# Routed two-of-eight expert kernel: a load gate tied to a gather's issue, and two single-tile scatter-adds moved behind gathers

## The chip, the cores and the metric

The kernel runs on one NeuronCore of a Trainium2 chip. The metric is device time of one execution in microseconds (us). Before the change it is 449.95 us, the median of three runs (449.35 to 451.89 us).

## What is computed

There are 4096 tokens (64 sequences of 64) of 256 numbers each. For every token a gate picks two of eight experts and gives each a weight; an expert is three dense layers (256 to 512, 512 to 512, 512 to 256), the first two with a relu. The output is the token plus the weighted sum of its two experts. The reference computes all eight experts for all tokens and gives six of them the weight zero:

```
var = jnp.mean(x * x, axis=-1, keepdims=True)
xn = rms_w * (x * jax.lax.rsqrt(var + EPS))
gate = xn @ wg_W + wg_b + (genre_embed @ gg_W + gg_b)
gate_w = jax.nn.softmax(gate, axis=-1)
topk_w, topk_i = jax.lax.top_k(gate_w, TOP_K)
cw = jnp.sum(jax.nn.one_hot(topk_i, E, dtype=x.dtype) * topk_w[..., None], axis=-2)
h1 = jax.nn.relu(jnp.einsum('bsh,ehm->bsem', x, W1) + b1)
h2 = jax.nn.relu(jnp.einsum('bsem,emn->bsen', h1, W2) + b2)
out_e = jnp.einsum('bsen,enh->bseh', h2, W3) + b3
return x + jnp.einsum('bseh,bse->bsh', out_e, cw)
```

(The last line joins the reference's last sum and its residual.) All arithmetic here is in float32.

## The kernel before, in words

**Tiles and units.** The kernel computes only the chosen pairs of token and expert. Pairs of one expert are collected in tiles of 128 token rows. Units 0 to 7 are single tiles, one for each expert, filled from the first 1024 tokens; they run while the other 3072 tokens are still being routed. From unit 8 (`E` in the code) on, a unit is up to four tiles of one expert, and its layers 1 and 2 are computed with seven block products in place of eight (class `Fast`); unit 8 is the first unit of four.

**What a unit needs.** Its rows of `x` come by an indirect DMA that GpSimd (POOL) issues, one for each tile (`gather` for units 0 to 7 into `xg`, `gather_unit` from unit 8 on into `xgE` or `big`; line 864). One more indirect DMA per tile fetches the eight gate weights of each token (`gather_cw`, tile `cg`, line 864), from a small array in DRAM (`cwdA` for units 0 to 7, `cwdR` from unit 8 on) that POOL wrote before (line 444); these are the column gathers of the change. Expert weights come by DMAs on SyncE's queue (SP) for the first units: layer 1 in the ring `w1r`, layer 2 in `w2a`, which keeps all eight experts, layer 3 in the ring `w3r`. From unit 8 on the rows go by SP through DRAM to be transposed: `stow` writes them to `scr` (line 904), `shuffle` reads them back into `gTs` (line 911), and VectorE (DVE) transposes blocks of `gTs` into `xT` (line 920).

**What a unit gives.** `give` scales the unit's result into `ys` or `xg` on DVE (line 1328) and adds each tile to the output rows in DRAM with an indirect DMA on POOL, the scatter-add (line 1329). Before any adds the output must hold the residual: `fill(k)`, k from 0 to 3, copies a quarter of the remaining rows of `x` to the output with a DMA of 768 KB on SP (line 1428). A scatter-add reads a row and writes it back, so each one waits until the scatter-adds of the unit before it have landed (the loop over `behind`); the first one of unit 8 waits for all fills too.

**The order.** The program is written out by hand in the order of each engine (`manual_schedule`). `first_part`, `gather(0)`, `other_loads`, `gather(1)` and `second_part` follow each other; then come `head_step(u)` for units 0 to 6, `step(7)`, and `step_fast(u)` from unit 8 on. Each engine takes its instructions in this order, so an instruction that waits holds all that stand behind it on its engine. Two waits concern the change:

- In `other_loads` (line 573) the first load on SP, `loads[2]`, which is layer 1 of expert 1 into `w1r`, waits until the first gather (`fetches[0]`, the rows of unit 0) has landed. All other weight loads stand behind it on SP.
- The `give` of unit 5 stands at the end of `head_step(6)`, that of unit 6 at the end of `step(7)`. Unit 8's column gathers (`gather_cw(8)` in `step(7)`) stand behind the first on POOL, unit 10's row gathers (`fetches_of(8)` in `step_fast(8)`) behind the second. `fill(3)` stands ahead of unit 10's `stow` on SP and waits for the last of unit 8's column gathers (`columns[E]`).

Of the kernel before, what the change touches and what calls it, by code (L numbers as in the profile page):

```python
# [11 lines left out]
F32 = mybir.dt.float32  # L12
# [3 lines left out]
ALU = mybir.AluOpType  # L16
# [36 lines left out]
def kernel(  # L53
# [53 lines left out]
    orows = out.rearrange("b s h -> (b s) h")  # L107
# [16 lines left out]
    def ring(pool, shape, tag, bufs, b, dt=F32):  # L124
# [32 lines left out]
        out=tri, in_=ones16, pattern=[[1, P]], compare_op=ALU.is_gt, fill=0.0, base=0, channel_multiplier=-1  # L157
# [4 lines left out]
        out=ntri, in_=ntri, pattern=[[1, P]], compare_op=ALU.is_ge, fill=0.0, base=0, channel_multiplier=-1  # L162
# [31 lines left out]
    idxR = const.tile([P, NREST], I32, name="idxR")  # L194
    ebt = const.tile([P, 1], I32, name="ebt")
    nex = const.tile([P, 1], I32, name="nex")
    vT = const.tile([P, 2, E, MC], F32, name="vT")


# [252 lines left out]
    fills, loads, fetches, fetched = [], [], [], []  # L452
# [119 lines left out]

    def other_loads():


        load_weights(1, (0,))
        tc.add_manual_dep(
            loads[2].ins,
            fetches[0].ins.name,
            mybir.DependencyInfo(mybir.DependencyClass.Sync, mybir.DependencyReason.DATA),  # L580
            reason="the first tile's rows go first",
        )
        load_weights(0, (2,))
        load_weights(1, (1,))
        load_weights(2, (0,))
        nc.sync.dma_start(b3_sb[:, 0:2], b3[0:2].unsqueeze(0).to_broadcast([P, 2, H]))
        load_weights(1, (2,))
        load_weights(2, (1,))
# [270 lines left out]
    def index(b):  # L859
        return idxA[:, b : b + 1] if b < E else idxR[:, b - E : b - E + 1]  # L860

    def fetch(dst, src, b):

        return nc.gpsimd.indirect_dma_start(  # L864
            out=dst,
            out_offset=None,
            in_=src,
            in_offset=bass.IndirectOffsetOnAxis(ap=index(b), axis=0),
            bounds_check=NT - 1,
            oob_is_err=False,  # L870
        )
# [13 lines left out]
            fetches.append(fetch(xgR[u % 2][:, k], xrows, b))  # L885

    NCG = 16
    columns = {}
    cgR = buf(run, [P, NCG, E], "cg")

    def gather_cw(u):
        for k, b in enumerate(tiles(u)):
            cg = cgs[b] = cgR[:, turn_of(u, k) % NCG]
            columns[u] = fetch(cg, (cwdA if b < E else cwdR)[:, :], b)

    xT = buf(run, [P, HC, SLOTS, BT], "xT")
    shs = gTf.rearrange("p (s k f) -> p s k f", s=SLOTS, k=P // SQ)
# [415 lines left out]
        n = rows(u, k)  # L1313
        nc.tensor.matmul(sums(u, k)[0:n], lhsT=(quad if n == SQ else both), rhs=y_of(u, k), start=True, stop=True)

    def give(u, which=None, summed=False, written=False):

        bs, cws = tiles(u), ww[u][4]
        if u not in given:
            given[u] = 0  # L1320
            adds.append([])
        for k in which or range(size(u)):
            b = bs[k]
            cw, bc = cws[k]
            n = within(u, k).stop - k * BT
            y = y_of(u, k)
            src = y if summed else sums(u, k)
            V.scalar_tensor_tensor(y[0:n], src[0:n], cw[0:n], bc[0:n], ALU.mult, ALU.add)  # L1328
            add = nc.gpsimd.indirect_dma_start(  # L1329
                out=orows,  # L1330
                out_offset=bass.IndirectOffsetOnAxis(ap=index(b)[0:n], axis=0),
                in_=y[0:n],
                in_offset=None,
                bounds_check=NT - 1,
                oob_is_err=False,
                **({} if written else {"compute_op": ALU.add}),
            )
            if reads and not written:
                tc.declare_no_dep(add.ins, reads[0].ins, reason="the tiles of a unit are of one expert: no token twice")
            if b < E:  # L1340
                for f in fills[1:]:
                    tc.declare_no_dep(add.ins, f.ins, reason="the first E tiles hold tokens of the first part alone")

            behind = list(adds[-2]) if len(adds) > 1 else [fills[0]]
            if b >= E and not behind_fills:
                behind += fills[1:]
                behind_fills.append(b)
            for a in adds[-1]:
                tc.declare_no_dep(add.ins, a.ins, reason="the tiles of a unit are of one expert: no token twice")
            for a in behind:  # L1350
                tc.add_manual_dep(
                    add.ins,
                    a.ins.name,
                    mybir.DependencyInfo(mybir.DependencyClass.Sync, mybir.DependencyReason.DATA),
                    reason="a token's row is read and written back",
                )
            adds[-1].append(add)
            given[u] += 1
        if given[u] == len(bs):
            ww.pop(u)  # L1360

    given = {}
    reads = []
    behind_fills = []
    NF = 4

    def head_step(u, more):

        if u + 3 < E:
            gather(u + 3)  # L1370
        for k in range(3 * u, min(3 * u + 3, E)):
            gather_cw(k)
        table(GC * (NCH - 1) * (u == E - 2))
        layer1(u)
        if u == 0:
            load_weights(u + RING, (0,))
            fills.append(nc.sync.dma_start(our[:, 0:NA, :], xr[:, 0:NA, :]))
            load_weights(u + RING - 1, (2,))
            load_weights(u + RING, (1,))
            nc.sync.dma_start(b3_sb[:, 2:4], b3[2:4].unsqueeze(0).to_broadcast([P, 2, H]))  # L1380
            third_part()
        elif u + RING < E:
            load_weights(u + RING, (0,))
        if u == 0:
            pass
        else:
            transpose_x(u + 1)
            stage_1(u + 1)
            if u == E - 2:
                while not fetched:  # L1390
                    more(1000000)
            elif u != 2:
                more(3200)
            if u > 1:
                scaled(u - 1, "A")
            layer3(u - 1)
            if u - 1 + RING < E:
                load_weights(u - 1 + RING, (2,))
            if u + RING < E:
                load_weights(u + RING, (1,))  # L1400
            if u in (2, 4):
                nc.sync.dma_start(b3_sb[:, u + 2 : u + 4], b3[u + 2 : u + 4].unsqueeze(0).to_broadcast([P, 2, H]))
        table(GC * (u == E - 3))
        if u == 0:
            layer2(u, {1: last_upright, 2: lambda: transpose_x(1)})
            stage_1(1)
            more(3200)
        else:
            more(3200)
            layer2(u)  # L1410
        if u == 1:
            scaled(0, "A")
        if u == E - 2:
            stream_3(E, mybir.EngineType.SP)
            fill(1)
            stream_1(E + 1, mybir.EngineType.SP)
            stow(E + 1)
            shuffle(E + 1)
            give(u - 2)
        if u >= 1 and u != E - 3:  # L1420
            give(u - 1)
        if u == E - 3:
            stream_1(E, mybir.EngineType.SP)
            fill(0)

    def fill(k):
        i = NA + k * (NB // NF)
        f = nc.sync.dma_start(our[:, i : i + NB // NF, :], xr[:, i : i + NB // NF, :])
        for a in sum(adds, []):
            tc.declare_no_dep(f.ins, a.ins, reason="the first E tiles hold tokens of the first part alone")  # L1430
        if k == NF - 1:
            tc.add_manual_dep(
                f.ins,
                columns[E].ins.name,
                mybir.DependencyInfo(mybir.DependencyClass.Sync, mybir.DependencyReason.DATA),
                reason="the weight columns of the first unit go first",
            )
        fills.append(f)

    def fetches_of(u, last):  # L1440
        far = E + 1 < u + 2 < last
        if far:
            gather_unit(u + 2)
            stow(u + 2)
        return far

    def step(u, last):
# [9 lines left out]
            stage_2(u)  # L1457
        if u + 1 < last:
            gather_cw(u + 1)
        if u - 1 >= E:  # L1460
            scales(u - 1)
        if u < last:
# [23 lines left out]
        if u == E - 1:  # L1486
            stream_1(E + 2, mybir.EngineType.SP)
            stream_3(E + 1, mybir.EngineType.SP)
            fill(2)
        give(u - 1)  # L1490
        for _ in folds:
            pass

    def step_fast(u, last):

        if u == E:
            transpose_x(u)
            fill(3)
        far = fetches_of(u, last)
        follows = u + 1 < last  # L1500
        if follows:
            gather_cw(u + 1)
# [188 lines left out]
    with tc.manual_schedule():  # L1691
# [21 lines left out]
        for u in range(E - 1, CUT):  # L1713
# [7 lines left out]
            elif u == CUT - 1:  # L1721
                tc.switch_hint({e: arm for e in ENGS}, len(ARMS), "tail")
            steps(u, u + 1, E + NQT + 1)
    kept = (ww, ex, cgs, given)
    state = [{k: list(v) if isinstance(v, list) else v for k, v in d.items()} for d in kept]
    done = [list(a) for a in adds]
    for k in tc.Switch(arm, len(ARMS), hint="tail"):
# [39 lines left out]
```

## Time and profile before

| | us |
|---|---|
| median of 3 runs | 449.95 |
| the profiled execution | 448.42 |
| its span (first to last instruction) | 446.7 |
| TensorE matmul (PE) busy | 439.6 |
| TensorE weight load (PEld) busy | 409.2 |
| DVE busy | 368.4 |
| ACT busy | 240.0 |
| POOL busy | 279.4 |

The profiled execution has 1.72 us outside its span. In the views, a row of the timeline gives the start in us, the duration in us, engine, line and operation, output from input, and in brackets the idle time of the engine just before with what ended it. Rows of waits give total us, number and longest. Rows of DMA issues give KB and us from issue to landing. Rows of DMA queues give packets, MB, and the share of the 16 DMA engines' time. SPq and ACTq are the issuing side of DMAs; q0 carries what POOL issues, q1 what SP issues. Lines in the profile are those of the kernel before.

### The profile page before, as it was taken

What the parts mean: (1) busy time and instruction counts of PE and PEld (TensorE: products, weight loads), DVE (VectorE), ACT (ScalarE), POOL (GpSimd) and SP (SyncE); (2) the same over time, 40 slices, a digit from 0 to 9 for tenths busy, and PEclk for the clock granted to TensorE, in tenths of its full rate; (3) what the DMA queues carried; (4) which work ended last, traced back from release to release, by engine and by line L of the source; (5) the groups of instructions that cost most, each with busy time, mean ns of one, the idle gap of its engine ahead of it and who ended that gap; (6) DMA issues with size and microseconds to landing.
All of it is one profiled execution on the core that took longest, in us unless ns stands there. A gap on an engine that the chain in (4) does not pass through costs nothing. (4 is left out here: it accounts for less than half of the span.)

```text
span 446.7 us, 9272 instructions
## 1 busy us (share of the span) xinstructions
PE 439.6 (98%) x2967; PEld 409.2 (92%) x2967; DVE 368.4 (82%) x964; ACT 240.0 (54%) x569; POOL 279.4 (63%) x234
## 2 busy tenths in 40 slices
PE   8999999999999999999999999999999999999995
PEld 7699999989889898989899999999999889999994
DVE  6898995698897979797988888887877878889962
ACT  6745544346556564738274646464464465655561
POOL 7854435757887878485765556577647456664323
PEclk9999999999999999999999999999999999999998
DMA  8799999784865857372746464666656555666312
GB/s 311 271 358 385 366 365 380 247 239 133 244 128 160 154 149 164 79 189 70 166 93 141 107 132 111 131 181 135 141 142 141 143 148 104 175 175 169 72 15 50
DMA packets 76015, 78.89 MB, mean 177 GB/s; under 512 B 34991, under 2 KB 64018, under 8 KB 75828
## 3 DMA queue, kind: packets, MB, share of 16 engines
q1 hardware_dynamic: 49408, 43.29, 30.0%
q0 software_dynamic: 14912, 17.60, 22.5%
q10 hardware_dynamic: 11636, 17.32, 12.1%
q8 instruction: 25, 0.41, 0.4%
q14 instruction: 34, 0.28, 0.2%
HBM read 62.73 MB, written 20.12 MB: 185 GB/s over the span
## 5 line engine op out<-in xcount | busy, mean ns | idle before, releaser
L1329 POOL DMA_INDIRECT out_dram<-ys,idxR x59 | 95.7, 1622 | 87.3 <-DVE ys L1328 42.1
L1157 PE MATMUL pb<-hid,big 128*128 128x256 f32 (+7 forms) x456 | 83.4, 326 | 0.0
L1178 ACT ACTIVATE hid<-hid,bb 128x256 f32<-128x256 f32 (+12 forms) x152 | 72.5, 526 | 17.9 <-DVE hid L1175 8.2
L864 POOL DMA_INDIRECT cg<-cwdR,idxR x59 | 66.4, 1125 | 18.0 <-issue 17.4
L1157 PEld LDWEIGHTS pb<-hid,big 128*128 128x128 f32 x456 | 71.4, 191 | 4.7 <-issue 0.8
L1279 PE MATMUL pb<-w3r,hid 128*128 128x256 f32 (+1 forms) x256 | 60.7, 381 | 0.0
L1166 ACT COPY q1s<-pb 128x512 f32<-128x512 f32 (+7 forms) x57 | 27.2, 476 | 60.7 <-PE pb L1157 60.0
L1157 PE MATMUL pb<-mixB,big 128*128 128x256 f32 (+7 forms) x304 | 55.4, 325 | 0.0
L1166 ACT COPY big<-pb 128x512 f32<-128x512 f32 (+7 forms) x57 | 27.1, 476 | 52.3 <-PE pb L1157 52.3
L1157 PE MATMUL pb<-hotA,big 128*128 128x256 f32 (+7 forms) x304 | 52.3, 325 | 0.0
L1279 PEld LDWEIGHTS pb<-w3r,hid 128*128 128x128 f32 (+1 forms) x256 | 46.2, 189 | 6.1 <-issue 0.8
L1157 PEld LDWEIGHTS pb<-mixB,big 128*128 128x128 f32 x304 | 47.9, 191 | 2.6
L1157 PEld LDWEIGHTS pb<-hotA,big 128*128 128x128 f32 x304 | 47.2, 191 | 2.7
L1157 PE MATMUL pb<-mixX,iotx 128*128 128x256 f32 (+7 forms) x228 | 46.3, 326 | 0.0
L864 POOL DMA_INDIRECT xgE<-in_x_dram,idxR x31 | 34.9, 1127 | 11.4 <-issue 8.5
L1157 PEld LDWEIGHTS pb<-mixX,iotx 128*128 128x128 f32 x228 | 37.1, 191 | 2.5 <-ACT q1s L1166 0.2
L864 POOL DMA_INDIRECT big<-in_x_dram,idxR x28 | 32.4, 1157 | 8.5 <-issue 7.0
L1178 ACT ACTIVATE hid<-pb,bb 128x256 f32<-128x256 f32 (+7 forms) x76 | 27.5, 413 | 14.5 <-PE pb L1157 11.4
L1157 PE MATMUL pb<-xT,w1r 128*128 128x256 f32 (+7 forms) x152 | 30.8, 325 | 0.0
L1058 PE MATMUL pb<-hid,w2a 128*128 128x128 f32 x256 | 30.5, 276 | 0.0
L1058 PEld LDWEIGHTS pb<-hid,w2a 128*128 128x128 f32 x256 | 29.7, 192 | 0.7 <-ACT bc L1024 0.4
L920 DVE STREAM_TRANSPOSE xT<-gTs 128x256 f32<-128x256 f32 x55 | 29.0, 632 | 0.0
(341 smaller groups left out, 822.0 us busy)
## 6 DMA issues: line engine op xcount, KB each, us to landing
w3r<-in_L_cond_W_dram ACTq DMA_DIRECT2D x17, 512.0 KB, 5.3
w2a<-in_L_cond_W_dram SPq DMA_DIRECT2D x8, 1024.0 KB, 14.1
w1r<-in_L_cond_W_dram ACTq DMA_DIRECT2D x16, 512.0 KB, 3.5
w1r<-in_L_cond_W_dram SPq DMA_DIRECT2D x11, 512.0 KB, 10.0
w3r<-in_L_cond_W_dram SPq DMA_DIRECT2D x10, 512.0 KB, 11.3
big<-in_x_dram SPq DMA_DIRECT2D x8, 512.0 KB, 6.5
gTs<-scr SPq DMA_DIRECT2D x7, 512.0 KB, 4.8
out_dram<-in_x_dram SPq DMA_DIRECT2D x4, 768.0 KB, 7.1
```

The source lines that it names most:

```text
L864: return nc.gpsimd.indirect_dma_start(out=dst, out_offset=None, in_=src, in_offset=bass.IndirectOffsetOnAxis(ap=index(b), axis=0), bounds_ ...
L920: V.transpose(xT[:, :, s0 + k, :].rearrange("p c (b k) -> p k c b", b=SQ), shs[:, s0 + k].rearrange("p k (a c) -> p k c a", a=SQ),)
L1058: nc.tensor.matmul(ph, lhsT=w2[:, m, ts(n, P)], rhs=hid[0][:, m, 0:BT], start=(m == 0), stop=(m == MC - 1))
L1157: nc.tensor.matmul(bank[:, ts(n, self.w)], lhsT=w[:, c, ts(n, P)], rhs=x[:, c], start=new and n == 0 and c == 0, stop=n == HB - 1 and c == ...
L1166: nc.scalar.copy(self.q[(1, 6, 5).index(k)], self.tall(self.X if k == 5 else self.U))
L1178: nc.scalar.activation(out, src, AF.Relu, bias=ww[self.u][1][:, self.l, n : n + 1])
L1279: nc.tensor.matmul(sums(u, k)[0 : cols.stop - cols.start], lhsT=hid[1][:, n, cols], rhs=w3[:, n, :], start=(i == 0), stop=(i == MC - 1))
L1329: add = nc.gpsimd.indirect_dma_start(out=orows, out_offset=bass.IndirectOffsetOnAxis(ap=index(b)[0:n], axis=0), in_=y[0:n], in_offset=None ...
```

## The change

It has two parts, and the weights, the arithmetic and the number of DMAs stay the same.

**The load gate.** A new tile `shut` of one number per partition is set to zero on POOL (`memset`) between `gather(0)` and `gather(1)`, and `loads[2]` waits for this `memset` in place of the first gather's landing. Since POOL works in order, the `memset` ends behind the issue of the gather. Tiles declared behind `shut` lie a little higher in the on-chip memory.

**The scatter-adds.** `give` is split: the DVE part stays where it was, and the DMA part becomes `send`, which can be held. The `send` of unit 5 is held until `gather_cw(8)` has been issued in `step(7)`; that of unit 6 is held until unit 10's row gathers, `stow(10)` and `fill(3)` have been issued in `step_fast(8)`. There `fill(3)` now stands behind `fetches_of`, and its wait for `columns[E]` is gone.

```
+    shut = const.tile([P, 1], F32, name="shut")
...
     def other_loads():
+        sent = nc.gpsimd.memset(shut, 0.0)
         load_weights(1, (0,))
         tc.add_manual_dep(
             loads[2].ins,
-            fetches[0].ins.name,
+            sent.ins.name,
...
-    def give(u, which=None, summed=False, written=False):
+    def give(u, which=None, summed=False, written=False, held=None):
...
             V.scalar_tensor_tensor(y[0:n], src[0:n], cw[0:n], bc[0:n], ALU.mult, ALU.add)
-            add = nc.gpsimd.indirect_dma_start(
...
+            if held is None:
+                send(u, b, y, n, written)
+            else:
+                held.append((u, b, y, n, written))
...
+    def send(u, b, y, n, written):
+        if u not in opened:
+            opened[u] = True
+            adds.append([])
+        add = nc.gpsimd.indirect_dma_start(
...
         if u >= 1 and u != E - 3:
-            give(u - 1)
+            give(u - 1, held=held if u == E - 2 else None)
...
-        if k == NF - 1:
-            tc.add_manual_dep(
-                f.ins,
-                columns[E].ins.name,
...
         if u + 1 < last:
             gather_cw(u + 1)
+        while held:
+            send(*held.pop(0))
...
-        give(u - 1)
+        give(u - 1, held=held if u == E - 1 else None)
...
         if u == E:
             transpose_x(u)
+        far = fetches_of(u, last)
+        if u == E:
             fill(3)
-        far = fetches_of(u, last)
+        while held:
+            send(*held.pop(0))
         follows = u + 1 < last
         if follows:
             gather_cw(u + 1)
```

Line numbers of the changed kernel are higher by 1 to 12, and tile numbers by one. On POOL, behind the setup, `xg_209` is the target of unit 0's gather and `cw8A` the gate weights of the first 1024 tokens. Before:

```order
L301 IOTA xgE 64x2208 x2
L864 DMA xg_209<-in_x_dram,idxA 128x256
L864 DMA xg_210<-in_x_dram,idxA 128x256
L864 DMA xg_211<-in_x_dram,idxA 128x256
L441 TENSOR_TENSOR cw8A<-ohA,denA 128x64
```

The same place on POOL in the change:

```order
L302 IOTA xgE 64x2208 x2
L866 DMA xg_210<-in_x_dram,idxA 128x256
L576 MEMSET shut 128x1
L866 DMA xg_211<-in_x_dram,idxA 128x256
L866 DMA xg_212<-in_x_dram,idxA 128x256
```

One instruction is new; what stood behind it is one place further down.

On POOL where units 5 to 8 meet, the rows `out_dram<-ys,idxA` are the scatter-adds of units 4 and 5, `out_dram<-xg` those of units 6 and 7, `cg` the column gathers (of unit 8, then of unit 9), `xgE` the row gathers of unit 10, `big` those of unit 11. Before:

```order
L444 DMA cwdR<-cw8B 128x256
L1329 DMA out_dram<-ys,idxA 4096x256 x2
L864 DMA cg<-cwdR,idxR 128x8 x4
L1329 DMA out_dram<-xg_211,idxA 4096x256
L864 DMA xgE<-in_x_dram,idxR 128x256 x4
L864 DMA cg<-cwdR,idxR 128x8 x4
L1329 DMA out_dram<-xg_209,idxA 4096x256
```

The same place on POOL in the change:

```order
L445 DMA cwdR<-cw8B 128x256
L1341 DMA out_dram<-ys,idxA 4096x256
L866 DMA cg<-cwdR,idxR 128x8 x4
L1341 DMA out_dram<-ys,idxA 4096x256
L866 DMA xgE<-in_x_dram,idxR 128x256 x4
L1341 DMA out_dram<-xg_212,idxA 4096x256
L866 DMA cg<-cwdR,idxR 128x8 x4
L1341 DMA out_dram<-xg_210,idxA 4096x256
```

Unit 5's scatter-add moved behind four column gathers, unit 6's behind four row gathers.

On SP at the same time, `out_dram<-in_x_dram` are `fill(2)` and `fill(3)`, `scr` from `xgE` is `stow(10)`, and `gTs` behind it is `shuffle(10)`. Before:

```order
L981 DMA w3r_86<-in_L_cond_W_dram 128x4x256
L1428 DMA out_dram<-in_x_dram 128x1536 x2
L904 DMA scr_187<-xgE 128x16x64
L911 DMA gTs<-scr_187 128x4x256
L1715 TENSOR_LOAD nex
```

The same place on SP in the change:

```order
L982 DMA w3r_86<-in_L_cond_W_dram 128x4x256
L1438 DMA out_dram<-in_x_dram 128x1536
L905 DMA scr_188<-xgE 128x16x64
L1438 DMA out_dram<-in_x_dram 128x1536
L912 DMA gTs<-scr_188 128x4x256
```

`fill(3)` moved from ahead of `stow(10)` to between it and `shuffle(10)`. The instructions of PE, DVE and ACT stand in the order that they had.

More of the change, by code (lines that the diff above doesn't have):

```diff
@@ L578, in other_loads @@
             loads[2].ins,
-            fetches[0].ins.name,
+            sent.ins.name,
             mybir.DependencyInfo(mybir.DependencyClass.Sync, mybir.DependencyReason.DATA),
-            reason="the first tile's rows go first",
+            reason="the first tile's rows are asked for first",
         )
@@ L887 @@
     NCG = 16
-    columns = {}
     cgR = buf(run, [P, NCG, E], "cg")
@@ L893, in gather_cw @@
             cg = cgs[b] = cgR[:, turn_of(u, k) % NCG]
-            columns[u] = fetch(cg, (cwdA if b < E else cwdR)[:, :], b)
+            fetch(cg, (cwdA if b < E else cwdR)[:, :], b)
     xT = buf(run, [P, HC, SLOTS, BT], "xT")
@@ L1314, in joined @@
         nc.tensor.matmul(sums(u, k)[0:n], lhsT=(quad if n == SQ else both), rhs=y_of(u, k), start=True, stop=True)
-    def give(u, which=None, summed=False, written=False):
+    def give(u, which=None, summed=False, written=False, held=None):
         bs, cws = tiles(u), ww[u][4]
-        if u not in given:
-            given[u] = 0
-            adds.append([])
+        given.setdefault(u, 0)
         for k in which or range(size(u)):
@@ L1328, in give @@
             V.scalar_tensor_tensor(y[0:n], src[0:n], cw[0:n], bc[0:n], ALU.mult, ALU.add)
[L1329 to L1350, printed above, removed]
-                tc.add_manual_dep(
[L1352 to L1357, printed above, removed]
+            if held is None:
+                send(u, b, y, n, written)
+            else:
+                held.append((u, b, y, n, written))
             given[u] += 1
@@ L1360, in give @@
             ww.pop(u)
+    def send(u, b, y, n, written):
[3 more added lines that the diff above has]
+        add = nc.gpsimd.indirect_dma_start(
+            out=orows,
+            out_offset=bass.IndirectOffsetOnAxis(ap=index(b)[0:n], axis=0),
+            in_=y[0:n],
+            in_offset=None,
+            bounds_check=NT - 1,
+            oob_is_err=False,
+            **({} if written else {"compute_op": ALU.add}),
+        )
+        if reads and not written:
+            tc.declare_no_dep(add.ins, reads[0].ins, reason="the tiles of a unit are of one expert: no token twice")
+        if b < E:
+            for f in fills[1:]:
+                tc.declare_no_dep(add.ins, f.ins, reason="the first E tiles hold tokens of the first part alone")
+        behind = list(adds[-2]) if len(adds) > 1 else [fills[0]]
+        if b >= E and not behind_fills:
+            behind += fills[1:]
+            behind_fills.append(b)
+        for a in adds[-1]:
+            tc.declare_no_dep(add.ins, a.ins, reason="the tiles of a unit are of one expert: no token twice")
+        for a in behind:
+            tc.add_manual_dep(
+                add.ins,
+                a.ins.name,
+                mybir.DependencyInfo(mybir.DependencyClass.Sync, mybir.DependencyReason.DATA),
+                reason="a token's row is read and written back",
+            )
+        adds[-1].append(add)
     given = {}
+    opened, held = {}, []
     reads = []
@@ L1430, in fill @@
             tc.declare_no_dep(f.ins, a.ins, reason="the first E tiles hold tokens of the first part alone")
-        if k == NF - 1:
-            tc.add_manual_dep(
-                f.ins,
-                columns[E].ins.name,
-                mybir.DependencyInfo(mybir.DependencyClass.Sync, mybir.DependencyReason.DATA),
-                reason="the weight columns of the first unit go first",
-            )
         fills.append(f)
@@ L1723 @@
             steps(u, u + 1, E + NQT + 1)
-    kept = (ww, ex, cgs, given)
+    kept = (ww, ex, cgs, given, opened)
     state = [{k: list(v) if isinstance(v, list) else v for k, v in d.items()} for d in kept]
```

## Prediction

> **What bounds the kernel now.** I read first the stretches by stage (busy time of each engine in each; the columns stand in the first line):
>
> ```profile
> core 0: us, PE busy (x) PEld busy (x) DVE busy (x) ACT busy (x) POOL busy (x), PEclk, DMA share, GB/s
> 21.00:83.00 62.00, 61.96 (x532) 59.82 (x527) 52.03 (x180) 28.87 (x82) 31.58 (x29) 1.00 1.03 366
> 83.00:130.00 47.00, 47.00 (x249) 41.63 (x248) 38.92 (x86) 25.01 (x50) 34.78 (x32) 1.00 0.66 181
> 130.00:440.00 310.00, 310.00 (x2028) 292.27 (x2027) 260.35 (x626) 171.33 (x404) 193.76 (x147) 1.00 0.57 132
> ```
>
> From 21 us to 440 us PE is busy nearly all the time at the full clock (PEclk 1.00). The DMA engines are full too from 21 to 83 us (share 1.03), POOL from 83 to 130 us for three quarters (34.78 of 47). Since the ends of matmuls are modelled, I then asked the waits of PEld, PE's weight loads, which show real gaps:
>
> ```profile
> PEld pb L932 <- DMA xg<-in_x_dram,idxA: 0.8, 1, 0.8
> PEld pb L1247 <- ACT big L1256: 0.5, 2, 0.3
> PEld pb L1058 <- ACT bc L1024: 0.4, 1, 0.4
> ```
>
> So PE waits once for a transfer, for the first gather, 0.8 us; never for weights and never for a column gather. A gain can only come from waits of this size. Both edits remove waits of SP, POOL and DVE; what counts is which of these PE feels.
>
> **The load gate.** POOL's issue of the first gather, SP's release and PE's first use, from the timelines of POOL, SP and PEld, with the gather's time from issue to landing and the price of a one-column memset on POOL:
>
> ```profile
> 16.64 1.11 POOL L864 DMA_INDIRECT xg<-in_x_dram,idxA  x1 [0.76 <-DVE totA L570]
> 20.13 0.34 SPq L461 DMA_DIRECT2D w1r<-in_L_cond_W_dram  x1
> 20.15 0.31 PEld L932 LDWEIGHTS pb<-ident,xg 128*128 128x128 f32 x2 [0.83 <-DMA xg<-in_x_dram,idxA]
> xg<-in_x_dram,idxA POOLq DMA_INDIRECT x1, 3.5
> 0.35 0.10 POOL L1753 MEMSET const-float32-1.0<- 128x1 f32 x1
> ```
>
> The gather lands at 16.64 + 3.5 = 20.1, and SP and PE both start then. In the change POOL has issued it at 16.64 + 1.11 = 17.75, the memset takes 0.10, so SP starts at about 17.9: the whole stream of weights comes 2.2 us earlier. The two gathers behind it come 0.1 later; they are wanted by later units.
>
> What do 2.2 us bring? Weights were waited for only here (waits of ACT and DVE):
>
> ```profile
> ACT bc L1024 <- DMA b_sb<-in_L_cond_b_dram: 2.9, 2, 2.2
> DVE iotx L1109 <- DMA w1r<-in_L_cond_W_dram: 1.8, 1, 1.8
> 48.62 0.37 ACT L1061 ACTIVATE hid<-pb,vT 128x128 f32<-128x128 f32 x1 [0.53 <-PE pb L1058]
> 83.66 0.69 DVE L934 COPY xT<-pb 128x512 f32<-128x512 f32 x1 [1.93 <-PE pb L932]
> ```
>
> The first two go for the most part, but soon after either of them the engine waits for PE again (0.53 us at 48.62, 1.93 us at 83.66), so PE gains nothing: 0 us. PE's gap at L1058 names an ACT instruction that itself waited for no transfer, and stays.
>
> What may it cost? PE starts on the first gather with no slack, so a later landing is paid one for one. The nearest row is the one above, 3.5 us with nothing behind it; the other gathers of this kind, beside the stream, give the other end:
>
> ```profile
> DMA to landing us min/median/max: 3.5/4.9/6.3
> ```
>
> So the cost lies between 0 (nothing in the edit speeds the gather up, so no gain) and 6.3 - 3.5 = 2.8 us. To choose, I look at when the packets move, in the DMA queues from 20.2 to 21 us, in the digits of the DMA engines from 17.9 to 20.2 us (40 slices of 0.0575 us), and in the queues from 21 to 23 us:
>
> ```profile
> q0 software_dynamic: 21, 0.02, 8.5%
> ```
>
> ```profile
> DMA  4231002009394941992311001001000099956439
> q0 software_dynamic: 75, 0.24, 36.0%
> ```
>
> ```profile
> q0 software_dynamic: 46, 0.13, 45.1%
> q1 hardware_dynamic: 61, 0.25, 35.4%
> ```
>
> After SP's issue at 20.13 no packet of SP's queue moves until 21: a lag of 0.9 us or more. In the change its first packets then come at about 18.8 us. The first gather's burst stands in slices 9 to 20, 18.4 to 19.05 us; the stream meets its end and its count of completion. A POOL packet took 0.360 x 16 x 2.3 / 75 = 0.18 us there and 0.451 x 16 x 2 / 46 = 0.31 us beside SP's first loads, 0.13 more. For the two or so packets of each engine that are still to come I take +0.3 us, near the end with nothing beside it.
>
> The Trainium skill (DMA: Bandwidth & Descriptors, section "Queues, rings and completion order") speaks against this edit: each DMA engine serves its queues in turn, packet by packet, and an engine's completion count lands only after all its earlier writes, across queues. By it the whole gather would share; an estimate by the two packet times above, four packets of an engine by 0.13, is 0.5 us in place of 0.3, a sum of 448.7. The trace agrees in direction (0.31 us a packet against 0.18).
>
> **The scatter-adds.** POOL where the units meet, DVE's read of the columns, and the gap of PEld that follows (from the timelines):
>
> ```profile
> 86.75 1.63 POOL L1329 DMA_INDIRECT out_dram<-ys,idxA  x1 [0.30 <-issue]
> 92.60 2.00 POOL L1329 DMA_INDIRECT out_dram<-ys,idxA  x1 [4.22 <-DVE xg L1328]
> 94.91 1.29 POOL L864 DMA_INDIRECT cg<-cwdR,idxR  x1 [0.30 <-issue]
> 99.15 1.25 POOL L864 DMA_INDIRECT cg<-cwdR,idxR  x1 [0.30 <-issue]
> 102.64 1.40 POOL L864 DMA_INDIRECT xgE<-in_x_dram,idxR  x1 [0.30 <-issue]
> 101.76 0.15 DVE L1007 COPY cw<-cg 128x1 f32 x1 [1.30 <-DMA cg<-cwdR,idxR]
> 112.86 0.97 PEld L1247 LDWEIGHTS pb<-ohB,mixB 128*128 128x128 f32 x8 [0.28 <-ACT big L1256]
> ```
>
> Unit 5's scatter-add holds POOL for 4.22 us; I read that as waiting for unit 4's (86.75) to land, for the DVE instruction that the row names writes `xg`, not the `ys` that is added here. The column gathers stand behind it, and DVE waits 1.30 us for the last.
>
> In the change they go first, but they read what POOL has just written to DRAM at 85.83. How long that takes to be readable is shown by the same write for the first tokens, at a time of full DMA engines:
>
> ```profile
> 85.83 0.61 POOL L444 DMA_DIRECT2D cwdR<-cw8B  x1 [0.30 <-POOL cw8B L443]
> 21.99 0.63 POOL L444 DMA_DIRECT2D cwdA<-cw8A  x1 [0.29 <-POOL cw8A L443]
> 27.93 1.01 POOL L864 DMA_INDIRECT cg<-cwdA,idxA  x1 [3.95 <-DMA cwdA<-cw8A]
> ```
>
> That was 5.9 us, so the first column gather starts between 88.7 (no wait) and 91.8. The last starts 99.15 - 94.91 = 4.2 later, 92.9 to 96.0, and lands 101.76 - 99.15 = 2.6 after that, 95.5 to 98.6. DVE came to them at about 100: its 1.30 us go at either end. DVE is then 1.3 us ahead, and ACT behind it, whose lateness at 112.86 made PE wait 0.28. That gap may go; since the other gap at this line stays whatever this edit does, I take -0.2, between 0 and -0.3.
>
> Unit 5's scatter-add goes out at 94 to 97 in place of 92.6, unit 10's row gathers at 96.5 to 99.6 in place of 102.64 (one scatter-add of some 2.3 us stands ahead), unit 6's behind them; their readers are other scatter-adds on POOL, which PE never waits for. What comes of it on SP is a rival below.
>
> **Sum.** 448.42 (the profiled execution) + 0.3 - 0.2 = 448.5 us. The median of the runs is 1.5 us above that execution; on its scale 449.95 + 0.1 = 450.1 us (rounded up). A measurement of this kernel tells a change of about 0.5% (2.25 us) from none.
>
> **Rivals.**
>
> *The stream catches the first gather (slower).* If SP's queue takes the engines from the start of the gather's burst, it lands as the later gathers do: 4.9 to 6.3 us, so +1.4 to +2.8, less 0.2: 451.2 to 452.6 us. For it: PE has no slack there. Against: the lag of 0.9 us. It decides at a landing 2.5 us later than 20.1. Chance 0.12.
>
> *Unit 10's rows come late (slower).* `fill(3)` now stands ahead of `shuffle(10)`. Its rows, the transposes on DVE and PE's first use of them:
>
> ```profile
> 110.59 0.38 SPq L904 DMA_DIRECT2D scr<-xgE  x1
> 115.22 0.38 SPq L911 DMA_DIRECT2D gTs<-scr  x1
> 120.41 2.07 DVE L920 STREAM_TRANSPOSE xT<-gTs 128x256 f32<-128x256 f32 x4
> 124.93 0.84 PEld L1157 LDWEIGHTS pb<-xT,w1r 128*128 128x128 f32 x4
> out_dram<-in_x_dram SPq DMA_DIRECT2D x4, 768.0 KB, 7.1
> gTs<-scr SPq DMA_DIRECT2D x7, 512.0 KB, 4.8
> ```
>
> PE is delayed once `shuffle(10)` goes out later than 124.93 - 2.07 - 4.8 = 118.1. With row gathers 3.0 to 6.1 us earlier, `stow(10)` goes out at 104.5 to 107.6, and `shuffle(10)` 4.6 us later, 109 to 112, with at most 7.1 on top for the fill: 119.3. If the gathers came no earlier, 115.2 + 7.1 = 122.3, PE 4.2 us late: 454.3 us. Chance 0.05.
>
> *The weights were the bound after all (faster).* If PE's matmuls between 21 and 83 us were stretched by late weights without showing a gap, the 2.2 us would come back, with 0.3 of the second edit: 447.5 us. For it: DMA engines full for 62 us. Against: no wait for weights in PE's rows. Chance 0.06.
>
> *Neither edit reaches PE.* The stream meets nothing, or the column gathers are held as long by their own write: 449.95 us. Chance 0.17.
>
> **Numbers.** The forecast has the remaining 0.60, from -0.3 to +0.6 around the median: 449.6 to 450.6. Together with "neither" that is 0.77; the median of a few runs moves too (449.35 to 451.89), so the range takes the first rival in part and ends at 448.7 and 452.0 us. Faster by over 0.5% (under 447.7): 0.05, most of the third rival. Slower by over 0.5% (over 452.2): 0.03 of the first rival and most of the second, 0.07. Within: 0.88.
>
> **What would show it.** Right: SP's load of `w1r` at about 17.9, PEld's wait for `xg` of 0.8 to 1.4 us, no wait of ACT for `b_sb` above 1 us, column gathers from 89 to 92 us on, no wait of DVE for `cg`, PE's stretches as full as before. Wrong: PE's wait for `xg` above 2 us; a wait of DVE's L920 for `gTs`; or PE reaching the transposes of unit 8 (L932 on `xgE`) more than 1 us earlier than before, which would say that weights had bound it.

## Result and the profile after

| | before | changed |
|---|---|---|
| median of 12 runs, us | 451.84 | 448.17 |
| lowest to highest, us | 449.35 to 454.05 | 447.65 to 448.75 |
| the profiled execution, us | 448.42 | 447.98 |
| its span, us | 446.7 | 446.3 |

The ratio is 0.9925, 95% interval 0.9905 to 0.9945: faster by 0.75%, and outside the range. Two things stand in the table. The two profiled executions differ by 0.44 us only; and the kernel before, whose profiled execution was faster than each of its 12 timed ones, lies 3.42 us above it in the median, the changed kernel 0.19 us above its own. The ratios here and below leave out executions of over 1.5% above the fastest of their kernel, so they can differ from the quotient of two medians.

The stretches of the changed kernel, with the columns of the prediction's first fence (its lines in the profile are 1 to 12 higher than before's):

```profile
21.00:83.00 62.00, 62.00 (x533) 60.34 (x530) 52.24 (x180) 28.97 (x83) 33.27 (x32) 1.00 1.02 362
83.00:130.00 47.00, 47.00 (x248) 41.82 (x247) 39.09 (x87) 25.42 (x51) 36.90 (x31) 1.00 0.71 191
130.00:440.00 310.00, 310.00 (x2029) 292.69 (x2028) 260.27 (x625) 170.61 (x403) 191.34 (x145) 1.00 0.56 130
```

PE was full and is full: in each stretch one matmul more or less. So the two profiles have to be compared by when the same matmul starts. Both have 2967 matmuls in one order; the changed kernel is ahead by 0.06 us from the first use of `xg` on, by 0.34 to 0.39 from unit 4's second layer on, by 0.54 from the gap at 112.86 us, by 0.76 from 316 us (a wait of 0.35 for DVE that is absent) to the last matmul; the spans end 0.4 us apart. Here are the rows behind these steps. The first gather: SP's release, the memset, PE's first use, and the DMA queues from 18.7 to 19.1 us:

```profile
17.92 0.34 SPq L462 DMA_DIRECT2D w1r<-in_L_cond_W_dram  x1
17.80 0.10 POOL L576 MEMSET shut<- 128x1 f32 x1
20.09 0.31 PEld L933 LDWEIGHTS pb<-ident,xg 128*128 128x128 f32 x2 [0.76 <-DMA xg<-in_x_dram,idxA]
```

```profile
q1 hardware_dynamic: 12, 0.04, 76.6%
q0 software_dynamic: 28, 0.06, 41.4%
```

The stream starts 2.2 us earlier and its packets (q1) do meet the gather's (q0), and yet PE starts at 20.09 in place of 20.15. Next the changed kernel's waits for weights (DVE, ACT), and PEld at unit 4's second layer in the changed kernel and in before:

```profile
DVE iotx L1110 <- DMA w1r<-in_L_cond_W_dram: 0.4, 1, 0.4
ACT bc L1025 <- DMA b_sb<-in_L_cond_b_dram: 0.3, 1, 0.3
```

```profile
52.95 1.75 PEld L1059 LDWEIGHTS pb<-hid,w2a 128*128 128x128 f32 x14
```

```profile
53.39 1.19 PEld L1058 LDWEIGHTS pb<-hid,w2a 128*128 128x128 f32 x10 [0.41 <-ACT bc L1024]
```

ACT's waits of 2.9 us for the biases are 0.3 now, and the gap of 0.41 that named an instruction of ACT (line 1024, which reads the biases) is gone. PE had not waited for that instruction: in the changed kernel PE starts at 52.95 while the same instruction runs until 53.25. Its rows, before first:

```profile
52.78 0.53 ACT L1024 ACTIVATE bc<-b_sb,cg 128x256 f32<-128x256 f32 x1
52.72 0.53 ACT L1025 ACTIVATE bc<-b_sb,cg 128x256 f32<-128x256 f32 x1
```

The trace also keeps the increments of the semaphores (counters that engines wait on) by which loads tell that they have landed. In before, PE's instruction stream stands at a wait of line 1058 for the semaphore of unit 4's layer-2 weights (`w2a`) until 53.32, and the last increment of that semaphore comes at 53.29. In the changed kernel the last increment comes at 51.57, ahead of PE's need. SP's rows of this load, before first:

```profile
39.02 1.49 SPq L461 DMA_DIRECT2D w2a<-in_L_cond_W_dram  x1
37.50 1.54 SPq L462 DMA_DIRECT2D w2a<-in_L_cond_W_dram  x1
```

So even in before's fast profiled execution PE waited once for weights, which is worth 0.28 us (from 0.06 ahead to 0.34), and it was close to it at other places: the layer-2 weights of units 2 and 3 landed 0.84 and 0.10 us ahead of PE's use. In the changed kernel these are 2.28 and 1.27 us, and every load of weights that PE uses between 21 and 80 us lands 1.27 us or more ahead of its use. Last the scatter-adds: column gather and held scatter-add on POOL, unit 10's rows on SP, PE at line 1248 and at unit 10's first matmul:

```profile
88.46 1.06 POOL L866 DMA_INDIRECT cg<-cwdR,idxR  x1 [1.50 <-DMA cwdR<-cw8B]
94.55 1.80 POOL L1341 DMA_INDIRECT out_dram<-ys,idxA  x1 [0.30 <-DVE iotx L1110]
103.49 0.38 SPq L905 DMA_DIRECT2D scr<-xgE  x1
108.18 0.37 SPq L912 DMA_DIRECT2D gTs<-scr  x1
112.21 1.08 PEld L1248 LDWEIGHTS pb<-ohB,mixB 128*128 128x128 f32 x8
124.39 0.62 PEld L1158 LDWEIGHTS pb<-xT,w1r 128*128 128x128 f32 x3
```

The column gathers start at 88.46, DVE's read of them at unit 8 waits no more, the gap of 0.28 at 112.86 is gone, and `shuffle(10)` goes out 7.0 us earlier (108.18 against 115.22). All that is 0.4 to 0.8 us. The other 3.2 us lie in executions of the kernel before that the profile does not show, and the experiments had to look for them.

### The profile page after: what moved, and what is told of

Same layout as the page of the kernel before. It is cut to its first block, busy times and chain, and to the rows that moved or that the text cites. A ratio compares the mean times of both kernels' runs of the same rounds, so it can differ in the third digit from the quotient of the medians.

```text
span 446.3 us, 9271 instructions
## 1 busy us (share of the span) xinstructions
PE 438.9 (98%) x2967; PEld 409.7 (92%) x2967; DVE 368.2 (83%) x964; ACT 239.9 (54%) x569; POOL 280.9 (63%) x235
## 5 line engine op out<-in xcount | busy, mean ns | idle before, releaser
L866 POOL DMA_INDIRECT cg<-cwdR,idxR x59 | 67.5, 1144 | 19.2 <-issue 17.1
```

What stands on the lines that cost most here:

```text
L866: return nc.gpsimd.indirect_dma_start(out=dst, out_offset=None, in_=src, in_offset=bass.IndirectOffsetOnAxis(ap=index(b), axis=0), bounds_ ...
```

## The experiments

They ran on other chips than the first pair (six are numbered in the results), each compared with the kernel before on the same chip at the same time. The theories: G, the earlier stream carries the gain; S, the scatter-adds carry it; A, the new tile's shift of the addresses. C, P, Q, N and M came later and are told where they start.

| label | kernel | chip | median, us (range) | before there | ratio (95%) | sd, us |
|---|---|---|---|---|---|---|
| e1_gate | gate alone | 3 | 464.19 (460.02 to 468.78) | 463.98 | 0.9977 (0.9935 to 1.0018) | 2.96 |
| e2_scatter | scatter-adds alone | 3 | 465.90 (461.69 to 468.18) | 463.98 | 1.0054 (1.0017 to 1.0092) | 1.88 |
| e3_tile | tile and memset alone | 3 | 464.31 (461.37 to 466.54) | 463.98 | 1.0016 (0.9983 to 1.0049) | 1.58 |
| e4_same | before | 3 | 464.88 (460.71 to 467.72) | 463.98 | 1.0021 (0.9981 to 1.0061) | 2.48 |
| n1_after | changed | 11 | 464.59 (460.85 to 466.13) | 464.16 | 0.9999 (0.9966 to 1.0032) | 1.54 |
| n2_gate | gate alone | 11 | 464.27 (461.63 to 467.68) | 464.16 | 1.0029 (0.9984 to 1.0073) | 2.17 |
| n3_scatter | scatter-adds alone | 11 | 465.78 (462.85 to 468.43) | 464.16 | 1.0028 (0.9995 to 1.0062) | 1.66 |
| n4_late | gate on 2nd gather | 11 | 464.84 (461.46 to 468.15) | 464.16 | 1.0086 (1.0037 to 1.0136) | 2.22 |
| p1_after | changed | 2 | 468.77 (465.94 to 471.41) | 469.55 | 0.9983 (0.9948 to 1.0017) | 1.73 |
| p2_gate | gate alone | 2 | 470.01 (465.49 to 473.82) | 469.55 | 0.9994 (0.9955 to 1.0032) | 2.58 |
| p3_scatter | scatter-adds alone | 2 | 469.20 (466.71 to 470.98) | 469.55 | 0.9995 (0.9968 to 1.0023) | 1.45 |
| p4_same | before | 2 | 469.47 (464.50 to 473.96) | 469.55 | 1.0017 (0.9982 to 1.0052) | 2.50 |
| z1_before | before, zeros | 9 | 465.45 (460.69 to 470.80) | 464.66 | 1.0000 (0.9959 to 1.0041) | 2.81 |
| z2_after | changed, zeros | 9 | 465.38 (463.38 to 467.54) | 464.66 | 1.0065 (1.0028 to 1.0101) | 1.25 |
| s1_gate | gate alone | 5 | 464.64 (459.19 to 467.25) | 465.16 | 0.9960 (0.9920 to 1.0000) | 2.68 |
| t1_scatter | scatter-adds alone | 15 | 467.05 (463.98 to 469.19) | 470.37 | 0.9925 (0.9890 to 0.9960) | 1.48 |
| t2_gate | gate alone | 15 | 469.37 (464.53 to 472.65) | 470.37 | 1.0003 (0.9963 to 1.0042) | 1.96 |
| v1_nocg | before, few column gathers | 11 | 453.12 (452.13 to 454.89) | 470.34 | 0.9667 (0.9621 to 0.9713) | |

(sd is the standard deviation of the kernel's 12 times, worked out from them; on the first chip it is 1.40 for before and 0.29 for the changed kernel. v1_nocg has 6 times.)

**Parts of the change.** e1_gate has the first half of the diff alone, e2_scatter the second half alone. e4_same is the kernel before itself, and e3_tile has of the diff only these two lines, with the old gate:

```
+    shut = const.tile([P, 1], F32, name="shut")
...
+        sent = nc.gpsimd.memset(shut, 0.0)
```

> The first edit alone: SP's loads wait for the memset behind the first gather's issue; scatter-adds and fill(3) stand as before. Theory G (the weight stream runs so close to PE's need that in most executions of the kernel before some load comes late, and its start 2.2 us earlier ends that): ratio to the kernel before 0.991 to 0.995 (448 to 450 us), and little spread between runs (about 1 us). Theory S (the held scatter-adds carry the gain: column gathers or row gathers come late in most executions): 0.999 to 1.001. Theory A (the tile shut moves the buffers behind it by 32 bytes, and that is what counts): as G.

> The second edit alone: scatter-adds of units 5 and 6 held, fill(3) behind unit 10's stow without its wait; the gate waits for the landing as before, and there is no tile shut. Theory G: 0.998 to 1.000 (the 0.2 to 0.3 us of DVE's wait for the columns at most), and as much spread between runs as the kernel before has (some 4 us). Theory S: 0.991 to 0.995 and little spread. Theory A: 0.999 to 1.001.

> The tile shut and its memset alone: they stand where the change has them, but the loads wait for the gather's landing as before. Theory G and theory S: 0.999 to 1.001 with the old spread. Theory A: 0.991 to 0.995.

> The kernel before, unchanged, for a second profile of it and for what a repeat gives. All theories: 0.998 to 1.002. Under theory G a profile of an execution that takes 451 us or more shows PE or ACT waiting for a load on SP's queue (w1r, w2a, w3r or b_sb) by some 2 to 4 us more than the first profile of the kernel before (448.42 us) did; under theory S it shows POOL or DVE waiting so long for the column gathers that PE has a gap of 2 us or more between 95 and 125 us.

None of them gained, e4_same's profile shows neither of the signs named for G and S (no wait of PE, DVE or ACT for a load of weights or biases, no gap of PE of 2 us from 95 to 125 us), and the kernel before takes 12 us longer on this chip than on the first (463.98 against 451.84). That rules out none of G, S and A, since it was not known whether the whole change gains anything here. So it ran itself, with its parts, and with the gate turned the other way (n4_late):

```
         gather(0)
+        gather(1)
         other_loads()
-        gather(1)
...
-            fetches[0].ins.name,
+            fetches[1].ins.name,
```

> The changed kernel itself, beside the kernel before on this chip. Theory G (the earlier stream of weights keeps PE from short waits in the stretch from 30 to 85 us, in most executions and not only in the profiled one): ratio 0.990 to 0.995, a narrow spread of times (about 1 us against 4 to 9). Theory S (the scatter-adds carry it): the same ratio. Theory C (the 0.75% belonged to one chip: its executions of the kernel before were disturbed by something that neither edit touches): 0.997 to 1.003 and a spread as wide as before's.

> The load gate alone, with the new tile and its memset; the scatter-adds as before. G: 0.990 to 0.996, close to the changed kernel of the same chip. S: 0.998 to 1.002. C: 0.997 to 1.003.

> The order of the scatter-adds alone; the load gate as before. G: 0.998 to 1.003. S: 0.990 to 0.996, close to the changed kernel of the same chip. C: 0.997 to 1.003; if 1.002 or more comes, this edit costs time by itself.

> The other way: the stream of weights is held until the second gather has landed (about 23 us, some 2.5 to 3 us later than before). G: slower, 1.004 to 1.008, as much as the earlier stream gained; in the profile PE waits longer at unit 4's first layer (0.4 us before) and for ACT's copy of the biases. The prediction's own view (no load is near PE's need, PE is the bound): 0.999 to 1.002. C: 0.997 to 1.003.

The changed kernel gains nothing here. In n4_late SP's load goes out at 21.18 us, 0.8 to 1.2 us later than with the old gate (19.95 to 20.43 us), less than the 2.5 to 3 expected. Its ratio of 1.0086 has the sign that G gave it, but the medians differ by 0.15% only, and in its profile every load of weights that PE uses between 21 and 80 us lands 1.83 us or more ahead of its use. What these chips share is in e4_same, the kernel before itself: POOL, ACT and PEld from 30 to 45 us:

```profile
29.87 0.99 POOL L864 DMA_INDIRECT cg<-cwdA,idxA  x1 [0.30 <-issue]
31.16 0.99 POOL L864 DMA_INDIRECT cg<-cwdA,idxA  x1 [0.30 <-issue]
32.46 0.99 POOL L864 DMA_INDIRECT xg<-in_x_dram,idxA  x1 [0.30 <-PE pb L1058]
33.76 1.05 POOL L864 DMA_INDIRECT cg<-cwdA,idxA  x1 [0.30 <-issue]
35.12 1.00 POOL L864 DMA_INDIRECT cg<-cwdA,idxA  x1 [0.30 <-issue]
36.42 1.13 POOL L864 DMA_INDIRECT cg<-cwdA,idxA  x1 [0.30 <-issue]
```

```profile
34.26 0.37 ACT L1061 ACTIVATE hid<-pb,vT 128x128 f32<-128x128 f32 x1 [3.93 <-PE pb L1058]
38.58 0.88 ACT L1061 ACTIVATE hid<-pb,vT 128x128 f32<-128x128 f32 x3 [3.96 <-remote]
```

```profile
34.87 0.53 PEld L1048 LDWEIGHTS pb<-xT,w1r 128*128 128x128 f32 x4
39.00 2.34 PEld L1048 LDWEIGHTS pb<-xT,w1r 128*128 128x128 f32 x12 [3.61 <-ACT hid L1061]
```

ACT waits 3.96 us for the end of PE's second layer, though PE was at the next layer from 34.87 on, and PE then waits 3.61 for ACT. In the first chip's profile the same matmuls run through. Stops of this kind stand in all the profiles of the kernels so far on these chips, mostly at the same few places: at 35 us, at 80 to 85 us, and in units 8 to 10, and the clock is halved behind the longer ones. That is theory C: the 0.75% belongs to stops of PE, not to either edit by itself.

The stops also hide what the load gate may do. While PE stands, the weights go on landing: in e4_same every load of weights that PE uses between 36 and 66 us lands 5.6 us or more ahead of its use, where the first chip's profile of before has 0.10 us at unit 3 and a wait at unit 4. A chip with these stops therefore cannot show what the earlier stream is worth on a chip without them.

> The changed kernel once more, on whatever chip comes. Theory C (PE is stopped for microseconds at a time, at the same places in both kernels and on some chips more than on others; the two edits themselves bring only the 0.41 us at unit 4 and the 0.28 us at unit 8): where the kernel before takes 460 us and more, 0.997 to 1.003; where it takes about 450 us, 0.992 to 0.999, and the profile shows the gaps at unit 4 and unit 8 gone. Theory G or S (an edit is worth 0.75% in itself): 0.990 to 0.995 wherever it runs.

> The load gate alone. C: within 0.3% of the kernel before on a chip of 460 us; on one of 450 us about 0.4 us less (ratio 0.999), unless the stops of PE differ. G: as the changed kernel, 0.990 to 0.995. S: 0.998 to 1.002.

> The order of the scatter-adds alone. It gave 1.0054 and 1.0028 on two chips before. C: 0.998 to 1.003. S: 0.990 to 0.996. G: 0.998 to 1.003. Above 1.002 a third time: the edit costs something by itself, which the gate makes up.

> The kernel before, unchanged, as one of the kernels: what ratio and spread come of nothing. 0.997 to 1.003; its profile on a chip of 450 us would show whether the executions of 452 to 454 us have stops of PE that the one of 448.4 us lacks.

A third chip, the same: all within 0.2% of before, as C says. That an edit, or the new tile, is worth 0.75% wherever it runs is out; what each is worth on a chip like the first is not.

**Is it the data?** z1_before and z2_after multiply the layers' inputs by zero and keep every instruction; one line of each kind:

```
-            nc.scalar.activation(hid[0][:, m, 0:w], ph, AF.Relu, bias=bb[:, 0, m : m + 1])
+            nc.scalar.activation(hid[0][:, m, 0:w], ph, AF.Relu, bias=bb[:, 0, m : m + 1], scale=0.0)
...
-            nc.scalar.copy(xT[:, :, s0, :], PB[4][:, 0 : HC * BT].rearrange("p (c t) -> p c t", c=HC))
+            nc.scalar.mul(xT[:, :, s0, :], PB[4][:, 0 : HC * BT].rearrange("p (c t) -> p c t", c=HC), 0.0)
```

> The kernel before with zeros in the matrix products: the copies of the transposed tokens into xT (units 0 to 7), the biases and every Relu are multiplied by 0, so the hidden layers are zero and the experts' outputs are left out (in units 9 and on the first layer still has its data). Instructions, transfers, waits and their order are the same. Theory P (PE's stops come from the array's work on real data): no stop of over 1 us at 35 us, and a ratio of 0.96 to 0.98 against the kernel before on a chip where that takes 460 us or more, with a spread of 1 to 2 us. Theory Q (the stops have to do with places in the program, not with data): the stops stay, ratio 0.995 to 1.003.

> The changed kernel with the same zeros. Against z1_before on the same chip: theory C (the edits bring only the gaps at unit 4 and unit 8, 0.7 us): 0.998 to 0.9995, so 0.2 to 0.9 us less, if the stops are gone in both. Theory G or S (an edit is worth 0.75%): 3 to 4 us less. If the stops stay (Q): as between the kernels themselves on such a chip, 0.996 to 1.004.

z1_before has the ratio 1.0000 and the spread of before, where P said 0.96 to 0.98. Its stop at 35 us is in parts of 0.84, 0.94 and 0.26 us, none over 1 us, as P said; but e3_tile has parts of 0.95 and 0.99 there without the zeros, z2_after has one of 2.44 with them, and from 120 to 135 us z1_before has gaps of 1.94, 2.52 and 3.21 us. P falls: the stops stay with most of PE's data at zero. The two medians, 465.45 and 465.38, show no gain of the change either.

**Late signals.** The trace keeps the increments of the semaphore by which PE tells that a matmul is done. I counted as late a signal for which no increment is recorded within 0.3 us after the end of its matmul (or 0.05 before it), and sorted PE's 1121 signals by whether POOL was at an indirect transfer (0.3 us either side):

```
                          at POOL's indirect transfers   elsewhere
                               late of signals         late of signals
before, first chip               0 of 848                 0 of 273
changed, first chip              0 of 837                 0 of 284
e4_same                        189 of 818                 1 of 303
n1_after                       188 of 822                 0 of 299
p4_same                        189 of 817                 4 of 304
z1_before                      188 of 815                 0 of 306
t1_scatter                     194 of 814                 5 of 307
v1_nocg                         96 of 580                 1 of 541
```

The other kernels on these chips have 178 to 207. That these signals come late, and are not only missing from the record, is seen in e4_same: matmuls that signal end at 35.14 and 35.58 us, no increment is recorded between 34.24 and 38.50, then four come up to 38.76, and ACT's wait of 3.96 us ends among them, at 38.58. POOL issues gathers one after the other up to 37.55 us, and ACT's wait ends 1.0 us behind that. The gate alone on a fifth chip:

> The load gate alone again, on its own. On a chip where the kernel before takes about 450 us: theory C 0.998 to 1.000 (0.4 us at unit 4, no more), with before spread as wide as the kernel; theory G 0.991 to 0.995; theory S 0.999 to 1.001 with the gaps at unit 8 still there. On a chip of 460 us and more: 0.996 to 1.003 by all that the other chips showed, with some 160 of PE's 1121 signals missing from the record.

It gave 0.9960 (0.9920 to 1.0000), with medians 0.11% apart and 156 signals without a record: one more of the same kind.

**The spread.** Up to here the kernels with the new order of the scatter-adds have sd 1.25 to 1.88 us (6 kernels), those with the old order 1.58 to 2.96 (9). That made theory N: the second edit takes away a variation between executions. It was put to the test:

> The order of the scatter-adds alone. Theory N (this edit takes away a variation from execution to execution): standard deviation of its 12 times 1.2 to 2.0 us where the kernel before has 2.2 to 2.8 on a chip of 460 us; on one of 450 us under 0.5 us against about 1.4, with a ratio of 0.992 to 0.995. Theory G: as wide as the kernel before, and 0.998 to 1.003.

> The load gate alone. N: as wide as the kernel before (standard deviation 2.2 to 3.0 us on a chip of 460 us, about 1.4 on one of 450 us), ratio 0.997 to 1.002. G: narrower than the kernel before by a third or more; on a chip of 450 us 0.991 to 0.995.

The scatter-adds alone: sd 1.48 beside 2.66 of before on this chip, as N says, and a ratio of 0.9925, for which N had no figure on such a chip. The gate alone: 1.0003, sd 1.96, a little under N's 2.2. So on this chip the second edit alone has the ratio of the whole change on the first; on chips 3, 11 and 2 it gave 1.0054, 1.0028 and 0.9995, so the equal figures may be luck. The traces show what it moves. Two rows of PEld, of p4_same (old order) and of t1_scatter (new order), at the same product of two neighbouring units:

```profile
156.32 1.59 PEld L1157 LDWEIGHTS pb<-hotA,big 128*128 128x128 f32 x8 [3.72 <-issue]
```

```profile
133.69 3.06 PEld L1156 LDWEIGHTS pb<-hotA,big 128*128 128x128 f32 x8 [5.66 <-issue]
```

In units 8 to 10 PE loses several us in every profile of these chips, most often at this product. With the old order most of it fell behind the 1000th matmul in 7 of 10 profiles and before it in 3; with the new order before it in 7 of 7. Between the matmuls that start at 85.0 and 163.7 us on the first chip, PE loses 3.8 to 10.9 us with the old order (mean 7.0) and 5.3 to 8.4 with the new one (mean 6.4): in these 17 profiles the new order narrows the loss and does not remove it.

**The cause of the stops by itself.** If POOL's indirect transfers hold the signals up (theory M), taking some away must give time back, although PE is the bound and POOL is not:

```
-            columns[u] = fetch(cg, (cwdA if b < E else cwdR)[:, :], b)
+            columns[u] = fetch(cg, (cwdA if b < E else cwdR)[:, :], b) if u == E else None
```

> The kernel before without the gathers of weight columns, but for the four of unit 8 (63 of POOL's 202 indirect transfers are left out; the columns that they would bring are zeros, so the experts' outputs are wrong; everything else is as before). Theory M (POOL's issue of an indirect transfer holds up the other engines' signals on such a chip): late signals of PE fall from 180 to 200 to about 130, PE's stop of 4 to 5 us at 35 us, where four column gathers follow each other, goes or halves, and the time falls by 4 to 8 us, ratio 0.983 to 0.992. Theory Q (the late signals have another cause and POOL is only busy most of the time): 180 to 200 late signals, the stop at 35 us stays, ratio 0.997 to 1.003. On a chip of 450 us: no late signals in either, 0.996 to 1.001.

453.12 us against 470.34, 17 us less, twice what M expected at most, and 97 late signals in place of the 130 expected. POOL and PEld of v1_nocg at the place of the first stop, and the stretches from 35.9 to 42.8 us of e4_same and of v1_nocg:

```profile
33.41 0.71 POOL L395 TENSOR_TENSOR wB<-gateB,prB 128x192 f32<-128x192 f32 x1 [5.14 <-DVE prB L387]
41.59 1.64 POOL L1329 DMA_INDIRECT out_dram<-ys,idxA  x1 [7.47 <-DVE pair L684]
```

```profile
34.70 1.87 PEld L1048 LDWEIGHTS pb<-xT,w1r 128*128 128x128 f32 x16
36.48 0.31 PEld L932 LDWEIGHTS pb<-ident,xg 128*128 128x128 f32 x2
```

```profile
35.90:39.40 3.50, 0.40 (x3) 0.40 (x4) 2.30 (x4) 0.82 (x4) 1.99 (x3) 0.99 1.02 407
39.40:42.80 3.40, 3.40 (x16) 3.22 (x16) 0.73 (x3) 2.43 (x8) 1.39 (x1) 0.50 1.06 367
```

```profile
35.90:39.40 3.50, 3.50 (x28) 3.20 (x27) 2.76 (x10) 1.85 (x6) 0.00 (x0) 1.00 1.02 412
39.40:42.80 3.40, 3.40 (x33) 3.40 (x32) 2.86 (x19) 1.35 (x4) 1.21 (x1) 1.00 1.05 379
```

No gather, no stop, and no halved clock behind it (PEclk 1.00 in place of 0.50), with the DMA engines as full as before (1.02 and 1.05). So on this chip the indirect transfers cost time although POOL is not the bound: Q is out, and M is right in direction and wrong in both sizes. That the way goes through the late signals is read from the rows at 35 us, where ACT waits for PE's signal. The kernel left out the gathers' data too, and with it DVE's and ACT's waits for the columns, so what one gather costs cannot be read from it. And it is the cause of the stops on these chips; the first chip's profiles have none of them.

## Why the prediction was wrong

**The steps that failed.** Two did. The larger is the last of the sum: "The median of the runs is 1.5 us above that execution; on its scale 449.95 + 0.1 = 450.1 us". It carried the distance between the profiled execution and the median, taken from three runs, over to the changed kernel as if it were a constant. Measured, it is 3.42 us for before over 12 runs and 0.19 us for the changed kernel. The other is the term of the load gate, worked out from "never for weights" and "so PE gains nothing: 0 us": PE did wait for weights, and +0.3 came out as a gain of 0.34 by unit 4's second layer. The sum, 448.5 for an execution like the profiled one, stands beside 447.98. With 447.98 and the old distance of 1.5 the time would have been 449.5, inside the range; so the distance decides. Of the 3.67 us between the medians, 0.44 lie in what the profiled executions show and 3.23 in the executions that they do not, and the cause of these 3.23 us stays open.

**The load gate, +0.3.** Wrong in sign, small in size. The stream did meet the gather as reckoned, at no cost: PE's wait went from 0.83 to 0.76. By the rule of turns between queues in the Trainium skill (DMA: Bandwidth & Descriptors, section "Queues, rings and completion order") the prediction made an estimate of 0.5 us for the same meeting. The row does not bear that out here, for the gather's landing. And "PE's gap at L1058 names an ACT instruction that itself waited for no transfer, and stays" was wrong: the row names the signal that came last, but PE needed the landing of unit 4's `w2a` at 53.29, and with the earlier stream the gap is gone. That this gap belongs to the gate is read from the loads' semaphores; no run on a chip like the first has the gate alone.

**The scatter-adds, -0.2.** Right as a mechanism and nearly in size: column gathers from 88.46 (said: from 89 to 92 on), no wait of DVE's read at unit 8 for `cg`, the gap of 0.28 gone, PE 0.15 us further ahead there. Missed was that this edit moves POOL's long runs of gathers against PE's work, which counts where they hold signals up.

**The rivals.** The first (the stream catches the gather) and the second (unit 10's rows late) did not happen: PE's wait for `xg` is 0.76, `shuffle(10)` went out at 108.18. The third, weights as the bound, gave 447.5 and is nearest to the time. Its mechanism holds in small: PE waited for weights, though with a gap that the rows show, and reached unit 8's transposes at 82.48 in place of 82.87, 0.4 us earlier and not 2.2; that the time came so near is luck as far as the profiles go. The list of what would show it was met nearly to the number; it was made for one execution, and most of the difference lay in others.

**What stays open.** Two readings of the 3.23 us are left, and neither is shown, since only before's fastest execution has a trace. By the first, the weights came later to PE in the slower executions of before: in the fastest they landed 0.10 us ahead of PE's use at one place and held it at another, and the changed kernel, with 1.27 us or more, has a spread of 0.29 us in place of 1.40. No run tests it. By the second, signals came late in those executions: for it speak the spread, which the second edit narrows elsewhere, and the 0.9925 of t1_scatter; against it, that the traced execution has no late signal, that this edit gave 0.9995 to 1.0054 on three chips, and that the whole change gained nothing on two. The gate alone and the scatter-adds alone on a chip that takes about 450 us would decide. Why some chips hold the signals up and others not stays open too.

## What to carry to other kernels

Before a predicted gain is put on the scale of a median, ask how far the profiled execution lies from that median, and whether the change touches what varies: here that was 3.23 us beside 0.44. A row that puts a wait down to a compute instruction can hide a load: ask whether the waiting instruction needed what is named, and when the load that it does need had landed. And an engine off the critical path, like POOL here with 63% busy time, can go with late signals of the others: where a profile has waits of ACT or PE that name a matmul long done, look whether POOL is issuing indirect transfers, and try with fewer of them.

## What the hardware showed beyond that

On six chips PE's signals came late almost only while POOL issued indirect transfers (178 to 207 of 1121 late with all of the transfers in place, at most 5 of some 305 outside), and about a seventh of the increments has no record of its own (953 to 971 recorded for 1121); on the first chip PE's signals stood 0.014 us (median) behind the matmuls' ends in both kernels. The same kernel took 451.84 us on the first chip and 463.98 to 470.37 on the others, and on chip 11 it took 464.16 at one time and 470.34 at another.

In e4_same the stop at 35 us is paid twice: PE has 0.40 us of work from 35.9 to 39.4 us, and from 39.4 to 42.8 the granted clock is 0.50. The Trainium skill (TensorE: Matmul & The Clock Gate, section "Part 1: The HAM clock gate") says that the clock is set by free-running windows of 3413 ns and halves after an idle one. The trace agrees with 3.41 us at half clock; the window before it was not wholly idle, but had 0.40 us of PE's work.
